# An attention and density kernel on one core: the values' offset written by ScalarE, later output stores, and a denser last stretch

## The chip, the core and the metric

The kernel runs on one core of a Trainium2 chip. TensorE (PE) multiplies matrices into PSUM; VectorE (DVE), ScalarE (ACT) and GpSimd (POOL) work element by element; SyncE (SP) issues nearly all DMAs here. Each engine works through its own instructions in order, and semaphores tie the engines together. The metric is the device time in microseconds (us) of one execution.

## What is computed

The input `x` has 8 images of 192 channels and 64 x 64 points. Layer 0 is attention over the 4096 points of an image, added to x; layer 1 is a per-channel density, added again:

```python
# layer 0, on g = group_norm(x)
q = prelu(conv1x1(g, w1, b1), a1)        # 24 channels
k = prelu(conv1x1(g, w2, b2), a2)        # 24 channels
v = prelu(conv1x1(g, wa, ba), aa)        # 192 channels: the "values"
score = softmax(q^T k, axis=2)           # 4096 x 4096
x = x + score @ v
# layer 1, on xr = group_norm(x), a small net per channel (1, 3, 3, 3, 1 units)
lower, upper = net(xr - 0.5), net(xr + 0.5)
sign = -sign(lower + upper)
x = x + maximum(abs(sigmoid(sign * upper) - sigmoid(sign * lower)), 1e-6)
```

All data is float32. A float32 matmul of the program shows as two records in the profile.

## The kernel before

**Steps.** An image's attention is 8 row blocks of 512 queries (n) by 16 steps; `t` counts the steps of all images, 1024 in all, `t % 16` is the step within a row block, and `b` is the image. In a step the loop at the end of the function calls `scores(t + 1)`: two matmuls (L802) into the one `sc` tile and, on ACT, the exponential (L806) into one of two `e` tiles. Then `max_step(t + 22)`: two matmuls (L729) and a maximum on DVE (L737) for a later row block. Then `attend(t)`: eight matmuls (L817, sixteen records) that add `e` times the values to the output of the row block. Then `work_off(t)` runs everything else. The last 22 steps have no `max_step` any more.

**Work written by hand into an order.** `at(t, fn, cost, act, pe)` puts a function into step t; `run_due` runs those that are due. What needs a PSUM bank is a `job`: `start_job` starts at most one a step when a bank of the tile in `homes` is free (the one of the two `turns` tiles b0 and b1, of two banks each, that `attend` is not adding into), from step 3 of a row block, and only when its hold fits before step 16. A job keeps its banks for `hold` further steps. Jobs are: `keys` (L641: queries and keys of 256 points), `values`, the output's transposes and residual (`finish`: L850, L859), the group norm (`norm_end`) and the folding of norm and weights (`weights`).

**Values.** A value job makes 256 points by 192 channels: two banks, three channel groups (L690, 64 rows each), and as a fourth product a row of ones times `ba`, the offset, which so reaches every point:

```python
for g in range(4):
    for s in range(2):
        ... lhsT=t[p, g, k * 128 : k * 128 + 128] if g < 3 else one_row[p],
            rhs=wf["v", b][p, g, :] if g < 3 else wf["ba", b][p],
```

One step later two activations on ACT (L617) and, after them, one DVE instruction (L620) make the prelu. An image has 16 value jobs; image 0's run in the head, before the steps, and those of image b + 1 mostly in the steps of image b. `wf["ba", b]` is made in `weights` from `ba_row`, which holds the offset in two of its 128 partitions (L200, L226, L587).

**SP's queue.** SP issues in order: loads of x for statistics, keys and values (`load`, L109, xi), of x for the residual (L109, xc, three tiles of 4 row blocks each), the keys' and queries' stores and reloads (L656, L657, L672), the row maxima (`max_end`: collected at step 9, `nd<-rn` L769 at step 11, `q<-nd` L774 at step 13, needed by the scores of the next row block) and the output (L1382). In `store` the DVE instruction that adds the density to xc (L1379) and the two output DMAs are in the same step; after an xc tile's last third its buffer is free, and a load that was held back for it follows in that step.

**Density.** 12 units an image (2 halves of the points x 3 channel groups x 2 bounds), each a list of instructions for DVE and ACT (L1102 `stt` on DVE; L1070, L1079, L1085, L1095 on ACT). `density_step` gives them out step by step against a credit on each engine; DVE's rate is what is left of the oldest image's units over the steps to its end plus 15, at most `MOST` = 3.3 us a step. `ending` joins two units and leads to `store`. After the last step image 6's rest is worked off, and image 7's units run with part of their sums on PE (L1041, the "tail"), some onto banks that ACT has filled (L1025).

**Head.** The x of image 0 is loaded, 14 matmuls of the identity (L146, tile `idle`) run meanwhile, then norm, keys and values of image 0.

Of the kernel before, what the change touches and what calls it, by code (L numbers as in the profile page):

```python
# [17 lines left out]
def kernel(  # L18
# [43 lines left out]
    nc = tc.nc  # L62
# [78 lines left out]
    make_identity(nc, ident)  # L141


    idle = ps_mx.tile([128, 2, F], F32, tag="mx", name="idle")
    for i in range(14):
        nc.tensor.matmul(  # L146
            idle[:, i % 2, 0:384], lhsT=ident, rhs=ident.unsqueeze(1).to_broadcast([128, 3, 128]),
            start=True, stop=True,
        )
# [27 lines left out]
    ba_row = const.tile([128, C], F32, name="ba_row")  # L177
# [3 lines left out]
    for t in (*wr, ba_row, one_row):  # L181
        nc.vector.memset(t, 0.0)
    nc.vector.memset(one_row[0:1], 1.0)
    nc.vector.memset(one_row[R : R + 1], 1.0)
# [10 lines left out]
    for s in range(2):  # L195
        p = slice(R * s, R * s + R)
        nc.scalar.dma_start(out=s1[p], in_=w1t.rearrange("(r g) o -> r g o", g=3))
        nc.scalar.dma_start(out=s2[p], in_=w2t.rearrange("(r g) o -> r g o", g=3))
        nc.scalar.dma_start(out=sa[p], in_=wat.rearrange("(r g) o -> r g o", g=3))
        nc.scalar.dma_start(out=sb[R * s : R * s + 1], in_=ba.unsqueeze(0))  # L200
    for i in range(2):
        for k in range(4):
            b_ = b2 if k // 2 == i else b1
# [8 lines left out]
    def spread():  # L212

        for i in range(2):
            for k in range(4):
                at = slice(32 * k, 32 * k + CR)
                p = slice(R * (k % 2), R * (k % 2) + R)
                nc.gpsimd.tensor_copy(wr[i][p, :, at], (s2 if k // 2 == i else s1)[p])
        for g in range(3):
            nc.gpsimd.tensor_copy(  # L220
                wa_sb[:, g, :].rearrange("p (h r) -> p h r", h=3),
                sa[:, g, :].rearrange("p (r h) -> p h r", h=3),
            )
        for s in range(2):
            p = slice(R * s, R * s + 1)
            nc.gpsimd.tensor_copy(  # L226
                ba_row[p].rearrange("p (h r) -> p h r", h=3),
                sb[p].rearrange("p (r h) -> p h r", h=3),
            )

    def negatives():
        for i, a in enumerate((*slope, vslope)):
# [101 lines left out]
    def at(t, fn, cost=0.0, act=0.0, pe=0.0):  # L334

        due.setdefault(max(t, now[0]), []).append((fn, cost, act, pe))
# [24 lines left out]
        ps_mx.tile([128, 2, F], F32, tag="mx", name="mx_head"),  # L361
    ]

    scratch = []
    for k in "ab":
        pair = []
# [5 lines left out]


    spot = [None]

    def spotted():

# [10 lines left out]
    def start_job(t):  # L388
        p = t % STEPS
        for n, (rank, make, hold, banks, cols) in enumerate(jobs):  # L390
            if stream[0] and (p < 3 or p + max(hold, 1) >= STEPS):
                continue
            rooms = [(pm, g) for pm, g in homes if sum(k <= t for k in g) >= banks]
            if not rooms:
                if rank < 2:
                    return
                continue
            k = [i for i in (1, 0) if ready[i] <= t and scratch[i][0].shape[1] >= cols]
            if cols and not k:
                continue  # L400
            del jobs[n]
            pm, guest = min(rooms, key=lambda r: max(r[1]))
            at_ = [i for i in range(2) if guest[i] <= t]
            for i in at_[:banks]:
                guest[i] = t + hold + 1
            if cols:
                ready[k[0]] = t + 2
            spot[0] = next(n for n, k in enumerate(turns + others) if k is pm), at_[0]
            parts = make(pm if banks == 2 else pm[:, at_[0], :], scratch[k[0]] if cols else None)
            for i, fn, cost, act, pe in parts:  # L410
                at(t + i, fn, cost, act, pe)
            return
# [50 lines left out]
    def norm_end(key, n, t, then=None):  # L463
# [68 lines left out]
                then()  # L532

        def make(pm, _):
            cell["pm"] = pm
# [12 lines left out]
    def weights(b, then):  # L548
# [41 lines left out]
        at(now[0] + 1, scale, 0.3, 2.0)  # L590

        def make(pf, _):
            cell["pf"] = pf
            cell["write"], cell["read"] = spotted()
            return [(0, products, 0.0, 0.0, 2.0), (1, offsets, 1.0, 0.0, 0.0)]
# [34 lines left out]
    def keys(b, d, what, done):  # L630
# [5 lines left out]
        def make(pk, u):  # L636
            if b not in kt:
                kt[b] = kpool.tile([128, N // 4], F32, tag="k", name=f"k_{b}")
            write, read = spotted()
            for g in range(3):  # L640
# [36 lines left out]

    def values(b, d, k, what, done):

        t = xi[what, b, d]  # L680
        c, h = divmod(d, 2)

        def make(pv, u):
            if (b, c) not in vt:
                vt[b, c] = vtiles.pop(0)
            v = vt[b, c][:, :, 2 * h + k, 0:C]
            for g in range(4):
                for s in range(2):
                    p = slice(R * s, R * s + R)
                    nc.tensor.matmul(  # L690
                        pv[:, s, 0:C],
                        lhsT=t[p, g, k * 128 : k * 128 + 128] if g < 3 else one_row[p],
                        rhs=wf["v", b][p, g, :] if g < 3 else wf["ba", b][p],
                        start=g == 0, stop=g == 3,
                    )
# [12 lines left out]

    rowmax = {}
# [118 lines left out]
    def finish(b, n, t):  # L828
# [17 lines left out]
        def turn():  # L846
            po = cell["po"]
            for k in range(2):
                for g in range(3):
                    nc.tensor.transpose(  # L850
                        po[:, g, k * 128 : k * 128 + 128],
                        o[k][:, g].rearrange("p s r -> p (s r)"), ident,
                    )

        u = slice((n % 4) * 256, (n % 4) * 256 + 256)
# [11 lines left out]
                norm_end((b, 1), 3 * NB, now[0] + 1, lambda: density(b))  # L867

        def make(po, _):
            cell["po"] = po.rearrange("p a (j c) -> p (a j) c", j=2)  # L870
            return [(0, turn, 0.0, 0.0, 1.3), (1, residual, 1.0, 0.0, 0.0)]

# [422 lines left out]
    def ending(b, c, g):  # L1295
# [80 lines left out]
        def store(parts=(slice(0, 2 * F),)):  # L1376
            for n in parts:
                x_ = xc[b, c][:, g, n]
                nc.vector.scalar_tensor_tensor(x_, z[0][:, n], 1e-6, x_, ALU.max, ALU.add)  # L1379
                for i in range(2):  # L1380
                    k = i * N // 2 + c * 2 * F
                    nc.sync.dma_start(  # L1382
                        out=ov[b, :, g, k + n.start : k + n.stop], in_=x_[R * i : R * i + R]
                    )
            bufs.append(z[0])
            if g == 2:
                xc.pop((b, c))
                free["xc"] += 1

# [134 lines left out]
    for t in range(last):  # L1524
# [9 lines left out]
                diagonals(2, last - 11)  # L1534
        now[0] = t
        if t % STEPS == 0:
            homes[:] = [(turns[(t // STEPS + 1) % 2], [0, 0])]
        if 3 < t < IMG:
            next(rest, None)
        assert t != IMG or next(rest, 0) == 0  # L1540
# [49 lines left out]
```

## Time and profile before

| what | value |
|---|---|
| median of 3 runs | 4759.76 us (4755.29 to 4764.86) |
| the profiled execution | 4759.02 us; its span 4757.2 us |
| mean granted TensorE clock | 0.985 |
| head: to the first L817 | 0 to 92.3 us |
| the 1024 steps | 92.3 to 4414 us |
| tail | 4414 to 4757 us |
| PE busy in 92 to 4414 us | 4301 of 4322 us |
| ACT and DVE busy in 92 to 4414 us | 2944 and 3775 us |
| SP's longest waits | L769 for DVE 1251.6 us in all, L1382 for DVE 894.8 us, L656 for DVE 671.3 us |

In the profile a group's line has the source line, engine, operation, what is written and read, the shape, the number of records, then busy time, the mean in ns of one, and the idle time just ahead with what ended it. A timeline line begins with the start and the duration in us. A window's line has the stretch, its length, then busy time and count for PE, PE's weight loads, DVE, ACT and POOL, the granted clock, the DMA share and GB/s. A wait of SP in its queue is often no more than SP being early.

### The profile page before, as it was taken

The page shows a single profiled execution, that of the slowest core. Times are in us where ns is not written, and L with a number is a line of the kernel's source. Part 1 is how long each engine was busy: PE and PEld are TensorE (multiplying, and loading weights), DVE is VectorE, ACT ScalarE, POOL GpSimd, SP SyncE. Part 2 cuts the span into 40 slices and gives each one's busy share as a digit, 9 for nine tenths or more (in the row PEclk, how much of TensorE's full clock was granted, in tenths as well). Part 3 has the DMA queues.
Part 4 walks back from the last instruction along what each step waited for, and adds up shares of the span by engine and source line. Part 5 has one row for each costly group of instructions (what it writes and reads, how often), then busy time and mean ns, then how long its engine had stood idle before and what let it go on. Part 6 is the DMA issues. An engine that isn't in the chain of part 4 may idle for free.

```text
span 4757.2 us, 68763 instructions
## 1 busy us (share of the span) xinstructions
PE 4609.7 (97%) x28116; PEld 3403.4 (72%) x28116; DVE 4125.5 (87%) x4161; ACT 3218.6 (68%) x3687; POOL 869.8 (18%) x841
## 2 busy tenths in 40 slices
PE   8999999999999999999999999999999999999685
PEld 5777777777777777777777777777777777777332
DVE  5433359999999999999999999999999998998898
ACT  2333247777677767877777767777777777778786
POOL 0000001222122212321212312222222222232100
PEclk9999999999999999999999999999999999999797
DMA  2101010111100111110111111111111101001000
GB/s 62 39 19 30 19 45 18 36 24 33 47 22 25 38 40 34 28 34 19 36 47 25 30 41 36 24 29 33 36 36 36 24 23 27 10 6 23 9 14 14
DMA packets 144145, 139.25 MB, mean 29 GB/s; under 512 B 51410, under 2 KB 116948, under 8 KB 143828
## 3 DMA queue, kind: packets, MB, share of 16 engines
q1 hardware_dynamic: 142592, 134.47, 12.1%
q8 instruction: 221, 3.62, 0.4%
q14 instruction: 96, 0.79, 0.1%
q10 hardware_dynamic: 1236, 0.37, 0.0%
HBM read 101.10 MB, written 29.49 MB: 27 GB/s over the span
## 4 chain that ended last, share of the span: by engine, by line
PE 89%; DVE 5%; ACT 3%; DMA 2%; issue 1%; SPq 0%; POOL 0%; ACTq 0%; POOLq 0%; DVEq 0%
PE b L817 57%; PE sc L802 21%; PE b L690 4%; DVE d L1102 3%; PE b L641 2%; PE b L1041 1%; PE mx L729 1%; DMA q<-nd 1%; PE mx_tail L1041 1%; PE b L850 1%; DVE rm L737 1%; DMA out_dram<-xc 0%; ACT d L1095 0%; PE sc_tail L1041 0%; SPq L109 0%
## 5 line engine op out<-in xcount | busy, mean ns | idle before, releaser
L817 PEld LDWEIGHTS b<-v,e 128*128 128x128 f32 x16384 | 2651.8, 190 | 777.8 <-issue 767.2
L817 PE MATMUL b<-v,e 128*128 128x193 f32 x16384 | 2955.6, 334 | 0.0
L806 ACT ACTIVATE e<-sc 128x1024 f32<-128x1024 f32 x1024 | 1044.7, 1020 | 1333.2 <-PE mx L729 1300.1
L737 DVE TENSOR_REDUCE rm<-mx 128x1 f32<-128x1024 f32 x1002 | 1224.1, 1222 | 511.6 <-PE mx L729 499.3
L802 PE MATMUL sc<-q,k 25*128 25x512 f32 x4096 | 1157.7, 641 | 23.6 <-DMA q<-nd 17.6
L729 PE MATMUL mx<-k,q 24*128 24x512 f32 x4008 | 1131.6, 641 | 0.0
L1102 DVE SCALAR_TENSOR_TENSOR d<-d,lc,d 128x1024 f32<-128x1024 f32 x756 | 977.3, 1301 | 17.2 <-ACT d L1079 4.8
L1102 DVE SCALAR_TENSOR_TENSOR d<-d,wsp,d 128x1024 f32<-128x1024 f32 x684 | 877.6, 1285 | 45.3 <-ACT d L1095 36.3
L1285 POOL MEMSET pause<- 128x1 f32 x408 | 40.0, 98 | 3560.9 <-DVE d L1102 3560.9
L1102 DVE SCALAR_TENSOR_TENSOR d<-d,tf,d 128x1024 f32<-128x1024 f32 x540 | 685.2, 1291 | 1.9 <-ACT d L1085 1.8
L1085 ACT ACTIVATE d<-d 128x1024 f32<-128x1024 f32 x540 | 567.2, 1052 | 38.0 <-DVE d L1102 37.7
L802 PEld LDWEIGHTS sc<-q,k 25*128 25x128 f32 x4096 | 308.1, 183 | 253.3 <-issue 205.8
L1095 ACT ACTIVATE d<-d,cb,wsp 128x1024 f32<-128x1024 f32 x348 | 429.9, 1235 | 1.5 <-DVE d L1102 0.6
L1070 ACT ACTIVATE d<-xc,bn,wn 128x1024 f32<-128x1024 f32 x288 | 354.2, 1234 | 0.8 <-issue 0.8
L1133 POOL TENSOR_TENSOR d<-d,d 128x512 f32<-128x512 f32 x168 | 340.9, 2029 | 45.9 <-ACT d L1127 44.8
L1079 ACT ACTIVATE d<-xc,bn,wn 128x1024 f32<-128x1024 f32 x252 | 311.1, 1234 | 0.0
L729 PEld LDWEIGHTS mx<-k,q 24*128 24x128 f32 x4008 | 300.0, 183 | 8.1 <-DVE rm L737 7.5
L1332 POOL TENSOR_TENSOR d<-d,d 128x512 f32<-128x512 f32 x80 | 172.5, 2156 | 0.0
L1320 POOL TENSOR_TENSOR d<-d,d 128x512 f32<-128x512 f32 x80 | 167.2, 2091 | 0.0
L1340 POOL TENSOR_TENSOR d<-d,d 128x512 f32<-128x512 f32 x80 | 159.5, 1994 | 2.0 <-POOL pause L1285 0.3
L690 PE MATMUL b<-wv,xi 64*128 64x192 f32 x1344 | 139.5, 340 | 0.0
L690 PEld LDWEIGHTS b<-wv,xi 64*128 64x128 f32 x1344 | 106.5, 186 | 25.4 <-issue 25.2
(156 smaller groups left out, 2176.9 us busy)
## 6 DMA issues: line engine op xcount, KB each, us to landing
xi<-in_x_dram SPq DMA_DIRECT2D x280, 192.0 KB
xc<-in_x_dram SPq DMA_DIRECT2D x64, 384.0 KB
out_dram<-xc SPq DMA_DIRECT2D x94, 256.0 KB
q<-qd SPq DMA_DIRECT2D x128, 128.0 KB
k<-kq SPq DMA_DIRECT2D x64, 64.0 KB
qd<-kq SPq DMA_DIRECT2D x64, 64.0 KB
q<-nd SPq DMA_DIRECT2D x256, 2.0 KB
d<-in_x_dram SPq DMA_DIRECT2D x16, 192.0 KB
```

The source lines that it names most:

```text
L690: nc.tensor.matmul(pv[:, s, 0:C], lhsT=t[p, g, k * 128 : k * 128 + 128] if g < 3 else one_row[p], rhs=wf["v", b][p, g, :] if g < 3 else wf ...
L729: nc.tensor.matmul(sc[:, s, :], lhsT=tile_of(qt[b, n // 2], n, j)[r], rhs=kt[b][r, u : u + F], start=True, stop=True,)
L737: nc.vector.tensor_reduce(out=rowmax[b, n][:, j, k : k + 1], in_=sc, axis=AX.XY, op=ALU.max)
L802: nc.tensor.matmul(sc[:, s, :], lhsT=kt[b][r, k : k + 128], rhs=qt[b, n // 2][r, :, u : u + 256], start=True, stop=True,)
L806: return lambda: nc.scalar.activation(e, sc, AF.Exp)
L817: nc.tensor.matmul(a[:, j, 0 : C + 1], lhsT=e[:, s, j * 128 : j * 128 + 128], rhs=v[:, s, p % 4, :], start=p == 0 and s == 0 and j % 2 == ...
L1070: nc.scalar.activation(self.buf[k], self.src(), AF.Tanh, bias=bn[:, s, g, 0, i : i + 1], scale=wn[:, g, 0, i : i + 1],)
L1079: nc.scalar.activation(self.buf[k], self.src(), AF.Identity, bias=bn[:, s, g, 1, i : i + 1], scale=wn[:, g, 1, i : i + 1],)
L1085: nc.scalar.activation(self.buf[k], self.buf["l", k[1], k[2]], AF.Tanh)
L1095: nc.scalar.activation(self.buf[k], self.buf["l", n - 1, 0], AF.Identity, bias=offset, scale=wsp[:, g, w : w + 1],)
L1102: nc.vector.scalar_tensor_tensor(dst, src, factor, dst, ALU.mult, ALU.add)
L1133: return nc.gpsimd.tensor_tensor(z[:, n], z[:, n], dst[:, n], ALU.add)
```

## The change

Value jobs that are neither image 0's nor of the last quarter of an image's values (`at_once`) let ACT write the offset into both banks in one step; the products run a step later, three groups instead of four, and add to what stands there. The job holds its banks and scratch tiles a step longer, so `start_job` asks for a step more. Whether a product adds or overwrites depends on what earlier matmuls of the bank left, so `part` notes banks where it may not, the warming matmuls now touch all eight banks (16 of 512 columns, for 14 of 384), and the output's transposes set the start flag only once a bank. For ACT's write the offset must stand in all partitions: `ba_all` is loaded by one broadcast DMA. The output's DMAs of a `store` are issued two steps after its DVE instruction, up to 12 steps before the last; the buffer comes free then. In the last 22 steps DVE's density rate aims at 8 steps after the last and may reach 4.3.

```diff
-    idle = ps_mx.tile([128, 2, F], F32, tag="mx", name="idle")
-    for i in range(14):
-        nc.tensor.matmul(
-            idle[:, i % 2, 0:384], lhsT=ident, rhs=ident.unsqueeze(1).to_broadcast([128, 3, 128]),
...
-        nc.scalar.dma_start(out=sb[R * s : R * s + 1], in_=ba.unsqueeze(0))
+    nc.scalar.dma_start(out=sb, in_=ba.partition_broadcast(128))
...
+    for i in range(16):
+        pm = (turns + others)[i // 2 % 4]
+        nc.tensor.matmul(
+            pm[:, i % 2, :], lhsT=ident, rhs=ident.unsqueeze(1).to_broadcast([128, 4, 128]),
+            start=True, stop=True,
+        )
...
-            if stream[0] and (p < 3 or p + max(hold, 1) >= STEPS):
+            if stream[0] and (p < 3 or p + max(hold, 1) + (cols > P and hold) >= STEPS):
...
-                ready[k[0]] = t + 2
+                ready[k[0]] = t + 2 + (banks == 2 and hold)
...
-            cell["read"](nc.vector.tensor_tensor(d, ba_row, pf[:, 4 : 4 + C], ALU.subtract))
+            cell["read"](nc.vector.tensor_tensor(d, ba_all, pf[:, 4 : 4 + C], ALU.subtract))
...
+        at_once = what == "first" or what == "v" and c == ORDER[3]
...
+            both = {(spot[0][0], i) for i in range(2)}
+            onto = not at_once and not part & both
+            part.difference_update(both)
+
+            def offset():
+                if onto:
+                    nc.scalar.activation(
+                        pv[:, :, 0:C], wf["ba", b].unsqueeze(1).to_broadcast([128, 2, C]), AF.Copy
                     )
-            done()
+
+            def products():
+                for g in range(4 - onto):
...
+                            start=not onto and g == 0, stop=g == 3 - onto,
+                            skip_group_check=onto,
+                        )
+                done()
...
+            if at_once:
+                products()
+                return [
+                    (0, lambda: None, 0.0, 0.0, 1.4), (1, first, 0.0, 1.1, 0.0),
+                    (2, last, 0.62, 0.0, 0.0),
+                ]
             return [
-                (0, lambda: None, 0.0, 0.0, 1.4), (1, first, 0.0, 1.1, 0.0),
-                (2, last, 0.62, 0.0, 0.0),
+                (0, offset, 0.0, 0.55, 0.0), (1, products, 0.0, 0.0, 1.1),
+                (2, first, 0.0, 1.1, 0.0), (3, last, 0.62, 0.0, 0.0),
             ]
 
-        job(make, *((0, 1) if what == "v" else (k, 3)), 2, 2 * C)
+        job(make, 0 if at_once else 1, 1 if what == "v" else 3, 2, 2 * C)
...
-                for g in range(3):
-                    nc.tensor.transpose(
+                for g in (1, 0, 2):
+                    nc.tensor.matmul(
                         po[:, g, k * 128 : k * 128 + 128],
-                        o[k][:, g].rearrange("p s r -> p (s r)"), ident,
+                        lhsT=o[k][:, g].rearrange("p s r -> p (s r)"), rhs=ident,
+                        is_transpose=True, start=k == 0 and g > 0, stop=True,
...
+            if t + LEAD >= last:
+
+                rate = min(left * COST["DVE"] / (last + 8 - t) + OTHER, MOST + 1.0)
...
                 nc.vector.scalar_tensor_tensor(x_, z[0][:, n], 1e-6, x_, ALU.max, ALU.add)
-                for i in range(2):
...
+                if now[0] >= last - 12:
+                    send(n)
             bufs.append(z[0])
-            if g == 2:
+            if now[0] < last - 12:
+
+                at(now[0] + 2, send)
...
+        def send(n=slice(0, 2 * F)):
+            x_ = xc[b, c][:, g, n]
+            for i in range(2):
+                k = i * N // 2 + c * 2 * F
+                nc.sync.dma_start(
+                    out=ov[b, :, g, k + n.start : k + n.stop], in_=x_[R * i : R * i + R]
+                )
+            if g == 2 and now[0] < last - 12:
+                xc.pop((b, c))
                 free["xc"] += 1
```

More of the change, by code (lines that the diff above doesn't have):

```diff
@@ L141 @@
     make_identity(nc, ident)
-    idle = ps_mx.tile([128, 2, F], F32, tag="mx", name="idle")
-    for i in range(14):
-        nc.tensor.matmul(
-            idle[:, i % 2, 0:384], lhsT=ident, rhs=ident.unsqueeze(1).to_broadcast([128, 3, 128]),
-            start=True, stop=True,
-        )
     gavg = const.tile([128, 128], F32, name="gavg")
@@ L176 @@
     wa_sb = const.tile([128, 3, C], F32, name="wa_sb")
-    ba_row = const.tile([128, C], F32, name="ba_row")
+    ba_all = const.tile([128, C], F32, name="ba_all")
     one_row = const.tile([128, 128], F32, name="one_row")
@@ L180 @@
     nslope = const.tile([128, 3], F32, name="nslope")
-    for t in (*wr, ba_row, one_row):
+    for t in (*wr, one_row):
         nc.vector.memset(t, 0.0)
@@ L223, in spread @@
             )
[L224 to L229, printed above, removed]
+        nc.gpsimd.tensor_copy(
+            ba_all.rearrange("p (h r) -> p h r", h=3), sb.rearrange("p (r h) -> p h r", h=3)
+        )
     def negatives():
@@ L374 @@
     spot = [None]
+    part = set()
     def spotted():
@@ L534, in make @@
         def make(pm, _):
+            part.add(spot[0])
             cell["pm"] = pm
@@ L592, in make @@
         def make(pf, _):
+            part.add(spot[0])
             cell["pf"] = pf
@@ L639, in make @@
             write, read = spotted()
+            part.discard(spot[0])
             for g in range(3):
@@ L686, in make @@
             v = vt[b, c][:, :, 2 * h + k, 0:C]
[L687 to L694, printed above, removed]
-                    )
-            done()
+            both = {(spot[0][0], i) for i in range(2)}
[5 more added lines that the diff above has]
+                        pv[:, :, 0:C], wf["ba", b].unsqueeze(1).to_broadcast([128, 2, C]), AF.Copy
+                    )
+            def products():
+                for g in range(4 - onto):
+                    for s in range(2):
+                        p = slice(R * s, R * s + R)
+                        nc.tensor.matmul(
+                            pv[:, s, 0:C],
+                            lhsT=t[p, g, k * 128 : k * 128 + 128] if g < 3 else one_row[p],
+                            rhs=wf["v", b][p, g, :] if g < 3 else wf["ba", b][p],
+                            start=not onto and g == 0, stop=g == 3 - onto,
+                            skip_group_check=onto,
+                        )
+                done()
             first, last = prelu(
@@ L848, in turn @@
             for k in range(2):
-                for g in range(3):
-                    nc.tensor.transpose(
+                for g in (1, 0, 2):
+                    nc.tensor.matmul(
                         po[:, g, k * 128 : k * 128 + 128],
-                        o[k][:, g].rearrange("p s r -> p (s r)"), ident,
+                        lhsT=o[k][:, g].rearrange("p s r -> p (s r)"), rhs=ident,
+                        is_transpose=True, start=k == 0 and g > 0, stop=True,
+                        skip_group_check=True,
                     )
@@ L869, in make @@
         def make(po, _):
+            part.difference_update((spot[0][0], i) for i in range(2))
             cell["po"] = po.rearrange("p a (j c) -> p (a j) c", j=2)
@@ L1379, in store @@
                 nc.vector.scalar_tensor_tensor(x_, z[0][:, n], 1e-6, x_, ALU.max, ALU.add)
-                for i in range(2):
[L1381 to L1384, printed above, removed]
-            bufs.append(z[0])
-            if g == 2:
+                if now[0] >= last - 12:
+                    send(n)
+            bufs.append(z[0])
+            if now[0] < last - 12:
+                at(now[0] + 2, send)
+            elif g == 2:
+                xc.pop((b, c))
[5 more added lines that the diff above has]
+                    out=ov[b, :, g, k + n.start : k + n.stop], in_=x_[R * i : R * i + R]
+                )
+            if g == 2 and now[0] < last - 12:
                 xc.pop((b, c))
@@ L1536 @@
         if t % STEPS == 0:
-            homes[:] = [(turns[(t // STEPS + 1) % 2], [0, 0])]
+            n = (t // STEPS + 1) % 2
+            homes[:] = [(turns[n], [0, 0])]
+            if t >= 2 * STEPS:
+                part.difference_update((n, i) for i in range(2))
         if 3 < t < IMG:
```

## The prediction

> **What bounds the kernel now.** I read the shares and slices of the page first, then its chain, then the groups, then the timeline of PE and of SP's queue around the longest waits.
>
> ```profile
> span 4757.2 us, 68763 instructions
> PE 4609.7 (97%) x28116; PEld 3403.4 (72%) x28116; DVE 4125.5 (87%) x4161; ACT 3218.6 (68%) x3687; POOL 869.8 (18%) x841
> PE   8999999999999999999999999999999999999685
> PE 89%; DVE 5%; ACT 3%; DMA 2%; issue 1%; SPq 0%; POOL 0%; ACTq 0%; POOLq 0%; DVEq 0%
> ```
>
> PE is busy from 92 us to 4414 us (the 1024 steps), and the chain agrees: 89% PE, DMA 2%. In the timeline the sixteen L817 matmuls of a plain step start every 3.88 us, and a step with more PE work is longer by just that work. So a matmul taken out of the steps is time saved, and ACT or DVE work there is free while it has room. After 4414 us that no longer holds.
>
> ```profile
> L690 PE MATMUL b<-wv,xi 64*128 64x192 f32 x1344 | 139.5, 340 | 0.0
> L690 PE MATMUL b<-ba,one_row 64*128 64x192 f32 x512 | 62.9, 322 | 0.0
> L806 ACT ACTIVATE e<-sc 128x1024 f32<-128x1024 f32 x1024 | 1044.7, 1020 | 1333.2 <-PE mx L729 1300.1 <-PE sc L802 30.0 <-ACT d L1095 0.2
> L617 ACT ACTIVATE pra<-b 128x384 f32<-128x384 f32 x128 | 55.7, 492 | 14.9 <-DVE v L620 12.5 <-DVE kq L620 2.4
> L802 PE MATMUL sc<-q,k 25*128 25x512 f32 x4096 | 1157.7, 641 | 23.6 <-DMA q<-nd 17.6 <-ACT e L806 5.7
> ```
>
> 512 records carry the offset row: 128 jobs, 4 records each (a written f32 matmul shows as two). PE's real waits in the steps are for q<-nd. SP's queue and PE at one of them:
>
> ```profile
> 4010.45 1.16 SPq L1382 DMA_DIRECT2D out_dram<-xc  x2
> 4014.68 2.56 SPq L109 DMA_DIRECT2D xc<-in_x_dram  x4
> 4017.27 0.60 SPq L769 DMA_DIRECT2D nd<-rn  x1
> 4029.37 2.39 SPq L774 DMA_DIRECT2D q<-nd  x4
> ```
>
> ```profile
> 4024.09 2.88 PE L817 MATMUL b<-v,e 128*128 128x193 f32 x16
> 4032.65 1.30 PE L802 MATMUL sc<-q,k 25*128 25x512 f32 x2 [5.68 <-DMA q<-nd]
> ...
> 4034.75 4.09 PE L817 MATMUL b<-v,e 128*128 128x193 f32 x16
> ```
>
> The load of a new xc tile must wait until the store that frees it has landed (4010.45 to 4014.68). Behind it in SP's queue stand nd<-rn, whose data was ready at 4005.6, and q<-nd, which PE needs at 4027.
>
> **Part 1: two matmuls less in 84 value jobs.** 7 images x 16 jobs less 4 that keep the old form: 84 jobs (the changed kernel's built order has 84 activations b<-ba). Each loses 4 records. Price: in the head two value jobs follow each other at 55.36 and 56.76, so 16 records take 1.40 us, 0.0875 each, 0.35 us for four. Ends: 0.32 (the offset's four at 56.44, next job at 56.76) and 0.42 (47.11 to 47.53, other work next). I take 0.35, the mean of a whole job: 84 x 0.35 = **-29.4 us** (-27 to -35).
>
> In exchange ACT writes 128x384 from SBUF to PSUM 84 times. No row has it; the nearest are 0.49 us (L617, PSUM to SBUF) and 0.61 us (L557, SBUF to SBUF, 128x384). At 1024 columns the write to PSUM of L1025 takes 1.10 against 1.23 to SBUF (L1070), so I take 0.49, 41 us of ACT. It is hidden by ACT's idle time ahead of the exponentials, 1333 / 1024 = 1.3 us a step. The new waits: PE's products, one step later, wait for that write, with the next step's scores queued behind them; the write is emitted a whole step ahead, so it is done. The write itself waits for the bank's last reader, with density work and a later exponential behind it on ACT. From the end of an exponential to the start of the scores that need its bank there are 1.62 us in the median; in images 1 to 7, 38 of 799 steps without a value job have under 0.5 us. So some 84 x 38/799 = 4 late exponentials, at up to 1.1 us (the step at 683.2 us is 1.03 long over the rule): **+2 us** (0 to +8).
>
> **Part 2: output stores two steps later.** Reading the L817 starts, I collect what the steps beside a late q<-nd are too long by: at 1296 and 1307 us 6.84 + 1.44; at 4024 and 4035 us 6.78 + 1.21; at 2123 and 2129 us 1.82 + 1.68; at 1578, 2669, 3213 and 3757 us 1.51, 1.40, 1.38, 1.46. Together 25.5 us, more than the 17.6 of the wait row, because matmuls after a long wait run slow: above, L802 1.30 for 0.70 and L817 4.09 for 2.88; the granted clock is 0.5 for 6.83 us from 4030.4. (The Trainium skill, "TensorE: Matmul & The Clock Gate", Part 1, says the clock halves after about 3.4 us idle and returns after as long a busy stretch; here a gap of 1.57 us at 2127.8 also brought 3.41 us at 0.5, so the trace is harsher. By that rule this pair would be worth 1.7 us less.)
>
> In the built order all seven have store and load ahead of q<-nd in the last steps before it is due: emitted at step 10, 11 or 12 of 16, q<-nd at 13. In the changed order six of the seven come at 14, after q<-nd. The seventh (image 7) moves from ahead of nd<-rn to behind it, with its DVE work two steps old, so SP need not wait. One new pair stands ahead of nd<-rn (image 1, sixth row block, step 10), two steps earlier relative to its data than the one shown above. I count 1 us for these (0 to 8): **-24.5 us** (-25.5 to -17). What else moves: xc comes free two steps later, so (image 3) its load is issued at step 414 instead of 411 and the first residual of the tile waits for the next turn of the banks (step 419 for 414). Its next user, the evacuation into the two o buffers, is at step 433; nothing on PE waits. Key jobs shift, and their stores now stand at steps 11 and 12 in five row blocks of images 2 to 6; one such pair before the change (step 318) cost nothing.
>
> **Part 3: more density in the last 22 steps.** In the built order 54 density and ending instructions of DVE fall there for 48, and 265 instead of 271 DVE instructions after the steps: six x 1.2 us (their spacing back to back) = 7.3 us moved. They fit: DVE is busy 71.4 of the 88 us from 4326, ACT 71.6 of 88 and gets five more. In the tail:
>
> ```profile
> 4414.00:4757.00 343.00, 234.68 (x503) 99.80 (x501) 297.91 (x274) 248.86 (x245) 11.02 (x10) 0.85 0.05 13
> ```
>
> DVE (third figure) is busy 298 of 343 us, but the tail's chain is DVE for only some 40%, PE 31% and ACT for much of the rest. 0.4 x 7.3 = **-3 us** (-7.3 to +5, if ACT comes late in those steps).
>
> **Part 4: the head.** Warming matmuls: 28 records of 384 columns from 1.36 us, 0.64 each until the clock rises at 6.1, then 0.32. 32 of 512 columns take 0.853 and 0.427: 4.74 us for 5.6 of them, 11.3 us for 26.4, end at 17.4. The first useful matmul waits for DVE's statistics until 23.07: **0**, hidden by them; without that cover up to 16 us. Between 27 and 34 us PE ran at clock 0.5; were the later end to keep it full, L568, L573 and the first L641 would win 1.3 + 1.05 + 0.66 = 3 us; the gap of 5.7 us argues against it. (The same section's 3.4 us window says cold as well.) The offset read into 128 partitions is 98 KB more, at the head's 76 GB/s 1.3 us, partly beside other work: **+0.5** (-3 to +1.3). Transposes are as many as before: 0.
>
> **Sum** against the profiled execution (4759.0 us: span 4757.2 and 1.8 around it): -29.4 + 2 - 24.5 - 3 + 0.5 = -54.4, 4704.6; the median of the runs is 0.7 higher, so 4705.
>
> **The rivals.**
> - *The late q<-nd stays*: another SP entry (a key job's store at step 12, the pair of image 1) takes the store's place. For: SP serves in order, and key jobs shifted. Against: the precedent at step 318. Part 2 falls away: 4705 + 24.5 = 4730. 13%.
> - *ACT comes late, slower*: the write and the two relus of two value jobs in neighbouring steps push the exponential past its 1.62 us, PE waits in each of the 84. At 1.1 us each +92: 4705 - 2 + 92 = 4795. It turns the sign from (54.4 + 2) / 84 = 0.67 us a job. For: ACT works 4.24 of the 5.38 us of a value step and 3.28 of 4.09 in the others, and the write goes into the latter. Against: density's credit on ACT is cut by the write's 0.55. 5%. (By the skill's rule gaps of 1.1 us would not cool the clock; one of five short waits here did.)
> - *The products save nothing*: accumulating on ACT's data runs slower, or PE hides the pair elsewhere. Against: in the tail L1041 onto banks that ACT filled runs at the same 0.43 us spacing. 4734. 5%.
> - *Better*: the head stays warm, the tail takes all 7.3 us, value at 0.42: 4705 - 3.5 - 4.3 - 5.9 = 4691. 7%.
>
> **How the numbers follow.** Forecast 67%, a mild form of the ACT rival (half a microsecond or so a job, near no change) 3%. Low: -35.3 - 25.5 - 7.3 - 3 = -71, 4688. High: the first rival with +5 from the tail, 4735. 0.2% (9.5 us) is about what a measurement of this kernel can tell from no change. Slower by more: the ACT rival, 5%; within: its mild form, 3%; faster: the rest, 92%.
>
> **What would show it.** After: L690 b<-ba at 176 records, 84 ACT writes near 0.49 us; plain steps still 3.88 us, value steps 5.38 - 0.35 = 5.03; L802 waiting for q<-nd under 3 us in all; steps from 92 us end near 4360; tail near 340 us. Wrong if L802 waits for L806 by tens of us, if q<-nd waits persist, or if value steps stay at 5.38.

## The result, and the profile after

The changed kernel takes 4706.68 us, the median of four runs (4706.02 to 4707.86), the kernel before 4762.31 us beside it (4755.29 to 4767.1): a ratio of 0.9885, 95% interval 0.9868 to 0.9902. Forecast were 4705 us in a range of 4688 to 4735. The total is right, in part by luck: of its terms one was seven microseconds too small, the others together were nearly nine too favourable, so the errors cancel, and a dependence between the parts was not seen. The page of the profile after, shares and chain:

```profile
span 4704.1 us, 68114 instructions
...
PE 4576.1 (97%) x27784; PEld 3371.2 (72%) x27784; DVE 4109.5 (87%) x4160; ACT 3260.4 (69%) x3771; POOL 869.5 (18%) x840
...
PE 89%; DVE 5%; ACT 4%; issue 1%; DMA 1%; POOL 0%; SPq 0%; POOLq 0%; ACTq 0%; DVEq 0%
```

PE has 33.6 us less work and the span is 53.1 us shorter: more than the removed products went. In the chain DMA is down from 2% to 1%. Groups that answer to those shown of before (L704 is the former L690, L828 the exponential L806, L824 the scores L802):

```profile
L824 PE MATMUL sc<-q,k 25*128 25x512 f32 x4096 | 1154.5, 640 | 13.3 <-ACT e L828 11.8 <-DMA q<-nd 1.2
L828 ACT ACTIVATE e<-sc 128x1024 f32<-128x1024 f32 x1024 | 1045.6, 1021 | 1227.0 <-PE mx L751 1202.3 <-PE sc L824 22.9
L704 PE MATMUL b<-wv,xi 64*128 64x192 f32 x1344 | 139.5, 340 | 0.0
L696 ACT ACTIVATE b<-ba 128x384 f32<-128x384 f32 x84 | 41.4, 493 | 1.8
L704 PE MATMUL b<-ba,one_row 64*128 64x192 f32 x176 | 21.6, 322 | 0.0
```

The offset's records are down from 512 to 176, and ACT writes 84 times at 0.493 us. The wait for q<-nd ahead of the scores fell from 17.6 to 1.2 us; the wait for the exponential rose from 5.7 to 11.8.

I divide each profiled span at the starts of the first and of the last L817 group (after: L839), and inside the steps I compare the distance between the starts of two steps with the median of the steps that have the same other PE work.

| stage | before | after | difference |
|---|---|---|---|
| head | 92.3 | 93.0 | +0.7 |
| steps, first to last L817 | 4319.7 | 4276.3 | -43.4 |
| tail | 345.2 | 334.9 | -10.3 |

A value step went from 5.382 to 5.057 us, so 84 of them are 27.3 us. The seven stretches around a late q<-nd were 25.5 us too long before; after, all are at their usual length but the one at step 926, which keeps 1.45. This is SP's queue and PE there, the place that the prediction showed at 4010 us of before:

```profile
3969.80 0.38 SPq L791 DMA_DIRECT2D nd<-rn  x1
3970.24 1.16 SPq L1422 DMA_DIRECT2D out_dram<-xc  x2
3981.38 2.86 SPq L109 DMA_DIRECT2D xc<-in_x_dram  x4
3984.34 2.38 SPq L796 DMA_DIRECT2D q<-nd  x4
```

```profile
3986.58 2.88 PE L839 MATMUL b<-v,e 128*128 128x193 f32 x16
...
3991.31 0.89 PE L824 MATMUL sc<-q,k 25*128 25x512 f32 x2 [1.19 <-DMA q<-nd]
```

nd<-rn now leaves ahead of the store, as soon as its data is there. But the store, issued right behind nd<-rn, takes 11 us to land and not 4 (3970.24 to 3981.38, against 4010.45 to 4014.68 before; the last section comes back to it), and the load waits for it 9.9 us with q<-nd behind. At the other six places the pair stands behind q<-nd and PE waits for nothing.

What the steps gave back: at steps 408, 536, 664 and 792 there are 1.2 us each that were not there before (step 280 had them already), 4.8 us in all. On ACT's timeline at step 408:

```profile
1803.11 1.00 ACT L828 ACTIVATE e<-sc 128x1024 f32<-128x1024 f32 x1
1804.13 1.28 ACT L501 ACT_TABLE_LOAD   x1
1805.42 0.20 ACT L501 ACTIVATE sq<-ve 128x1 f32<-128x1 f32 x1
1805.64 1.28 ACT L1353 ACT_TABLE_LOAD   x1
1806.94 1.15 ACT L1353 ACTIVATE d<-d 128x512 f32<-128x512 f32 x2
1808.00 0.61 ACT L1355 ACTIVATE d<-d 128x512 f32<-128x512 f32 x1
1808.52 1.00 ACT L828 ACTIVATE e<-sc 128x1024 f32<-128x1024 f32 x1
```

```profile
1805.56 2.88 PE L839 MATMUL b<-v,e 128*128 128x193 f32 x16
1809.57 0.70 PE L824 MATMUL sc<-q,k 25*128 25x512 f32 x2 [1.13 <-ACT e L828]
```

The group norm's square root needs another table of functions: 1.28 us to load it and 1.28 to load the old one back, and in the new order both fall into the same step as an ending's tanh (L1353, L1355). Before, the square roots stood in these same steps, but the exponential came right behind them: it is the tanh that moved there. The exponential comes late; no write of the offset is near.

The tail, in the windows' view (busy us and count of PE, PE's loads, DVE, ACT and POOL, then clock, DMA share, GB/s), and the 22 steps ahead of it:

```profile
4372.00:4704.00 332.00, 228.32 (x499) 97.61 (x498) 287.52 (x267) 241.78 (x240) 6.33 (x8) 0.87 0.05 13
4284.00:4372.00 88.00, 88.00 (x466) 66.44 (x458) 79.85 (x65) 77.98 (x93) 25.23 (x24) 1.00 0.03 7
```

DVE and ACT are busy 80 and 78 of the 88 us, where it was 71 and 72; PE has no idle time there, so the moved work costs the steps nothing.

### The profile page after: what moved, and what is told of

It reads as the page before. It is cut to its first block, busy times and chain, and to the rows that moved or that the text cites. A ratio compares the mean times of both kernels' runs of the same rounds, so it can differ in the third digit from the quotient of the medians.

```text
span 4704.1 us, 68114 instructions
## 1 busy us (share of the span) xinstructions
PE 4576.1 (97%) x27784; PEld 3371.2 (72%) x27784; DVE 4109.5 (87%) x4160; ACT 3260.4 (69%) x3771; POOL 869.5 (18%) x840
## 4 chain that ended last, share of the span: by engine, by line
PE 89%; DVE 5%; ACT 4%; issue 1%; DMA 1%; POOL 0%; SPq 0%; POOLq 0%; ACTq 0%; DVEq 0%
PE b L839 58%; PE sc L824 22%; DVE d L1128 3%; PE b L704 3%; PE b L642 2%; PE b L1067 1%; PE mx L751 1%; PE b L873 1%; ACT d L1121 1%; ACT d L1111 1%; ACT e L828 1%; PE mx_tail L1067 0%; DVE rm L759 0%; ACT d L1105 0%; ACT d L1096 0%
## 5 line engine op out<-in xcount | busy, mean ns | idle before, releaser
L839 PEld LDWEIGHTS b<-v,e 128*128 128x128 f32 x16384 | 2647.7, 190 | 776.1 <-issue 767.8
L839 PE MATMUL b<-v,e 128*128 128x193 f32 x16384 | 2951.5, 334 | 0.0
L828 ACT ACTIVATE e<-sc 128x1024 f32<-128x1024 f32 x1024 | 1045.6, 1021 | 1227.0 <-PE mx L751 1202.3
L824 PE MATMUL sc<-q,k 25*128 25x512 f32 x4096 | 1154.5, 640 | 13.3 <-ACT e L828 11.8
L824 PEld LDWEIGHTS sc<-q,k 25*128 25x128 f32 x4096 | 306.4, 183 | 243.2 <-issue 199.2
L1105 ACT ACTIVATE d<-xc,bn,wn 128x1024 f32<-128x1024 f32 x252 | 310.9, 1234 | 0.0
L704 PE MATMUL b<-wv,xi 64*128 64x192 f32 x1344 | 139.5, 340 | 0.0
L1067 PE MATMUL b<-d,v 128*128 128x512 f32 x216 | 104.1, 635 | 30.2 <-ACT b L1051 26.7
```

Source lines behind the costliest of these rows:

```text
L704: nc.tensor.matmul(pv[:, s, 0:C], lhsT=t[p, g, k * 128 : k * 128 + 128] if g < 3 else one_row[p], rhs=wf["v", b][p, g, :] if g < 3 else wf ...
L824: nc.tensor.matmul(sc[:, s, :], lhsT=kt[b][r, k : k + 128], rhs=qt[b, n // 2][r, :, u : u + 256], start=True, stop=True,)
L828: return lambda: nc.scalar.activation(e, sc, AF.Exp)
L839: nc.tensor.matmul(a[:, j, 0 : C + 1], lhsT=e[:, s, j * 128 : j * 128 + 128], rhs=v[:, s, p % 4, :], start=p == 0 and s == 0 and j % 2 == ...
L1105: nc.scalar.activation(self.buf[k], self.src(), AF.Identity, bias=bn[:, s, g, 1, i : i + 1], scale=wn[:, g, 1, i : i + 1],)
```

## Experiments

Theory: the three parts do what the prediction says and add up; the queue's order decides on the late q<-nd. Rivals: ACT's write is paid after all; it is the time, not the order, of the stores that counts; the tail hides or does not hide the moved work. Times are medians, and ratios are to the kernel before, timed again beside each set (4760.2 to 4764.7 us); spans and steps come from the profiled execution of each.

**The three parts one by one.** First, the kernel before with the new `store` and `send` alone:

```diff
-                    nc.sync.dma_start(out=ov[...], in_=x_[R * i : R * i + R])
...
+                if now[0] >= last - 12:
+                    send(n)
...
+            if now[0] < last - 12:
+                at(now[0] + 2, send)
```

> The kernel before with the later output stores alone. Theory (each late q<-nd came from a store and load ahead of it in SP's queue, and only that): the excess of the seven stretches, 25.5 us, goes but for about 1.5 us, the 1024 steps take 4296 instead of 4320 us, plain and value steps keep 3.88 and 5.38 us, the tail keeps about 345 us; 4762 - 24 = 4738. Rival (the gap closed because the value jobs, and with them keys and loads, stand elsewhere): several of the seven waits stay; 4750 to 4762.

4736.14 us, ratio 0.9946 (0.9931 to 0.9961), steps 4296.7: as the theory said.

```profile
L802 PE MATMUL sc<-q,k 25*128 25x512 f32 x4096 | 1154.3, 640 | 6.8 <-ACT e L806 5.1 <-DMA q<-nd 1.4
```

The wait for q<-nd is 1.4 us instead of 17.6. Stretches of 3.3 us remain at step 926. Second, the changed kernel with the old stores and the old rate, that is the values alone:

```diff
-            if now[0] < last - 12:
-                at(now[0] + 2, send)
...
-            if t + LEAD >= last:
-                rate = min(left * COST["DVE"] / (last + 8 - t) + OTHER, MOST + 1.0)
```

> ScalarE's write of the offset with all that belongs to it (bank notes, warming matmuls, transposes, offset in all partitions), without the later stores and without the denser last stretch. Theory: 84 value steps of 5.06 instead of 5.38 us, 27.3 us less; waits for q<-nd of 15 to 28 us stay; tail near 345; 4762 - 27 = 4735, 4725 to 4742. Rival (the order of the value jobs also cures the late q<-nd): 4710 to 4718.

4789.6 us, ratio 1.0059 (1.0042 to 1.0076): slower than before, which neither theory allowed. The value steps are at 5.06 us as expected, so the 27 us are there. But the scores now wait 50.7 us for q<-nd. SP and PE at step 478, where before had 3.5 us too much and this has 8.6:

```profile
2106.15 1.12 SPq L1408 DMA_DIRECT2D out_dram<-xc  x2
2109.91 2.56 SPq L109 DMA_DIRECT2D xc<-in_x_dram  x4
2112.57 2.40 SPq L796 DMA_DIRECT2D q<-nd  x4
```

```profile
2111.37 2.88 PE L839 MATMUL b<-v,e 128*128 128x193 f32 x16
2119.85 1.39 PE L824 MATMUL sc<-q,k 25*128 25x512 f32 x2 [5.60 <-DMA q<-nd]
...
2122.04 4.70 PE L839 MATMUL b<-v,e 128*128 128x193 f32 x16
```

In before the store of this place left 9.1 us ahead of the step's L817 (2113.63 against 2122.73), here 5.2 us. In the built order the density's last DVE instruction on xc (L1408) stands one step later in row blocks 26 to 54 (named, here and in the expectations, by the row block whose queries q<-nd brings; it is issued in the one ahead), since the changed value jobs shift the order of the density around them. Ten stretches are 75.3 us too long, for 25.5. The steps nearly add up: 4319.7 - 27.3 + (75.3 - 25.5) + 4.8 for the four late exponentials = 4347.0; measured 4346.2.

Third and fourth, the rate alone on the kernel before, and the changed kernel without it (the same two lines added, or taken out):

```diff
+            if t + LEAD >= last:
+                rate = min(left * COST["DVE"] / (last + 8 - t) + OTHER, MOST + 1.0)
```

> The kernel before with the higher density rate in the last 22 steps alone. Theory A (the six moved VectorE instructions and their consequences explain the shorter tail, 345.2 to 334.9 us): steps unchanged at 4320 us, tail 335; 4752. Theory B (the rate is worth the 3 us of the prediction, the rest comes from where the density stands when the steps end): tail 341 to 343; 4759.

4750.44 us, ratio 0.9978 (0.9968 to 0.9987); the tail alone moved, from 345.2 to 335.8.

> The changed kernel without the higher density rate. Theory A (the rate made the tail shorter): tail 345, 4717. Theory B (it is worth 3 us): tail 338, 4710. Steps at 4276 us by both.

4722.16 us (4718.07 to 4725.36), ratio 0.9916 (0.9901 to 0.993), tail 345.4. By the tails the rate is worth 9.4 us alone and 10.5 with the other parts; by the medians 11.5 and 15.5, but 3 us of the latter lie in the head (96.0 us here, 93.0 in the changed kernel). The stores are not independent: alone they bring 26 us, with the values 4789.6 - 4722.2 = 67 us.

**Why the values alone are slower.** Three kernels for that. The kernel before with only the DVE instruction on xc one step later, values untouched:

```diff
-                later(2, store, 1.3)
+                later(3, store, 1.3)
```

> The kernel before, with the density's last DVE instruction on xc one step later and the store and the load with it; the values are as before (four products, no write by ACT). In the built order the pair then stands ahead of q<-nd at the same step as in the values-only kernel in row blocks 22 to 54. Theory A (it was this one step that cost the values-only kernel its gain, not the write by ACT): nine stretches of some 8 us each and the one at 926 remains: excess 75 to 86 us for 25.5, so 4810 to 4823. Rival B (the write by ACT or the changed order of the jobs makes q<-nd late): within 10 us of the kernel before, 4752 to 4772.

4822.89 us, ratio 1.0128 (1.0113 to 1.0143). One number, which changes no amount of work, costs 61 us:

```profile
L802 PE MATMUL sc<-q,k 25*128 25x512 f32 x4096 | 1165.7, 644 | 67.2 <-DMA q<-nd 60.7 <-ACT e L806 5.9
```

The wait for q<-nd is 60.7 us instead of 17.6, with no write by ACT in the kernel; the ten long stretches sum to 88 us. So that one step is what the values-only kernel lost by.

Next, values alone, stores at the old place, and only the freed xc tile announced two steps later, so that the load that waits for the store moves behind q<-nd:

```diff
-            if g == 2:
-                xc.pop((b, c))
-                free["xc"] += 1
+            if g == 2 and now[0] < last - 12:
+                at(now[0] + 2, leave)   # leave: the two lines above
```

> Only the value change of the kernel before, with the output stores in the step of their DVE instruction as before, but the xc tile counted as free two steps later, so that only the load that reuses it moves behind q<-nd. Theory A (q<-nd was held back by the load that waits in SP's queue for the store to land): the long stretches of the values-only kernel (78 us) go, 4789.6 - 70 = 4720, and L802 waits for q<-nd under 5 us in all. Rival B (the stores themselves, or their traffic, hold q<-nd back): 4760 to 4790, with q<-nd waits of 20 to 50 us.

4716.63 us, ratio 0.9903 (0.9889 to 0.9918):

```profile
L824 PE MATMUL sc<-q,k 25*128 25x512 f32 x4096 | 1154.5, 640 | 12.0 <-ACT e L828 11.8
```

No wait for q<-nd is left at all, at step 926 neither. It was the load, waiting at the head of SP's queue; the stores, still in the step of their DVE instruction, did no harm at these places.

Last, the stores alone on the kernel before, but one step later instead of two:

```diff
-                at(now[0] + 2, send)
+                at(now[0] + 1, send)
```

> The kernel before, with the output stores of the steps issued one step after their DVE instruction (not two). In the built order the store and the load that waits for it then still stand between nd<-rn and q<-nd in row blocks 22 to 54 of the steps, exactly as before; only at rows 18 and 50 (counted from 0) do they move behind q<-nd. Theory A (only the place in SP's queue counts, not the step in which the entry is written): the seven long stretches stay but the one at step 286 (8.3 us): 4762 - 8 = 4754, steps near 4311. Rival B (what counts is that the store comes later in time): most of the stretches shrink as with two steps, 4736 to 4742.

4753.26 us, ratio 0.9981 (0.9972 to 0.9991), steps 4311.2: the times that theory A gave, but by luck, since two things that it did not have cancel. Where the order of the queue is unchanged, SP does the same at the same time: in the last steps of row blocks 21 and 37 (L817 of steps 350 and 606) the starts of store, load and q<-nd, counted from that L817, agree with the kernel before within 0.03 us. Writing an entry a step later does nothing by itself; it has to pass another entry. The stretches at 286 and at 926, where the pair did pass an entry, went but for 0.7 us (15.6 us less; theory A had the first alone), and the five others grew by 7.5 in all. PE waits 0.2 to 0.9 us longer there: before, six transposes (L850, 0.65 us) stood ahead of the scores in each of these five steps, and in the new order they stand elsewhere, so PE comes sooner to a q<-nd that lands at about the same time (the scores start 4.4 to 4.9 us after the step's L817, before 4.7 to 5.1). After four of these waits, now 1.5 to 2.0 us and three of them under 1.3 before, L817 took 4.4 to 4.6 us instead of 2.88. The end on the clock below comes back to that.

**Is ACT's write hidden?** The changed kernel with each write made twice:

```diff
                     nc.scalar.activation(
                         pv[:, :, 0:C], wf["ba", b].unsqueeze(1).to_broadcast([128, 2, C]), AF.Copy
                     )
+                    # the same three lines again
```

> The changed kernel, with each of the 84 writes of the offset by ACT made twice (the second overwrites the first with the same numbers): 41 us more work on ACT in the steps, which no plan of the kernel counts. Theory A (ACT has room ahead of its exponentials, the writes are hidden): 4707 to 4714. Rival B (ACT is near its limit in these steps, every further half microsecond is paid): up to 84 x 0.49 = 41 us, 4735 to 4748.

4712.33 us (4709.62 to 4713.34), ratio 0.9892 (0.9875 to 0.9908):

```profile
L827 PE MATMUL sc<-q,k 25*128 25x512 f32 x4096 | 1155.3, 640 | 14.2 <-ACT e L831 11.8 <-DMA q<-nd 2.2
L699 ACT ACTIVATE b<-ba 128x384 f32<-128x384 f32 x84 | 41.5, 495 | 2.7
```

With the second write (L699) ACT works 41.5 us more, and the scores wait for the exponential 11.8 us as before. The steps are 3.4 us longer, 2.7 of them at step 926 for q<-nd; at most 0.8 us can be the writes'. The head of this execution was 3.1 us longer.

**More jobs in the new form.** The write also in the head:

```diff
-        at_once = what == "first" or what == "v" and c == ORDER[3]
+        at_once = what == "v" and c == ORDER[3]
```

> The changed kernel, with ACT writing the offset in the head's value jobs of image 0 too (16 more jobs, 100 writes in all). In the built order SP's queue in the steps is as in the changed kernel. Theory A (the head's value jobs are bound by PE's products there, as in the steps): 16 x 0.325 = 5.2 us off, 4701.5. Rival B (the head's end is set by other work, by DMAs or by ACT, which in the head has no idle exponentials to hide the write): 4706 to 4712.

4722.72 us, ratio 0.9914 (0.9901 to 0.9928): 16 us worse than the changed kernel, more than either theory had, and all of it in the head (109.2 us; steps 4275.4). The windows from 47 to 57 us, this kernel and then the changed one:

```profile
47.00:57.00 10.00, 9.40 (x42) 4.68 (x40) 6.94 (x8) 2.39 (x6) 0.00 (x0) 0.62 0.16 41
```

```profile
47.00:57.00 10.00, 9.75 (x82) 6.18 (x82) 8.78 (x10) 2.99 (x8) 0.00 (x0) 1.00 0.16 39
```

PE is busy in both, but at a granted clock of 0.62 it does half as many matmuls. From 45 us to the end of the head this kernel takes 64.2 us at a mean granted clock of 0.75, which is 48 us at full clock; the changed kernel takes 48.0 us at 1.00. So nearly all of the 16 us is the clock. In the head the write has no cover: near its end PE waits for it twice, 1.41 us each (98.0 and 101.7 us). Why the clock fell already at 49 us, after two waits of 0.5 and 0.6 us, stays open (the changed kernel has one of 0.7 there and keeps its clock).

The write in half of the last quarter's jobs as well (14 more), with the head's and then without:

```diff
-        at_once = what == "first" or what == "v" and c == ORDER[3]
+        at_once = what == "v" and c == ORDER[3] and h
```

> As the run with the head's jobs, and with the write also in half of the value jobs of the last quarter of each image: 14 more of them in the steps. The added step moves the density endings: in five row blocks (18, 26, 34, 42, 50) the store and its load stand ahead of q<-nd again, but their DVE instruction comes one step earlier than in the kernel before, where these rows cost nothing. Theory A (it is the time of that DVE instruction and the place in the queue that decide): no new wait, 14 x 0.325 = 4.6 us less than the run with the head alone. Rival B (any pair ahead of q<-nd costs 7 us or so): 30 to 40 us slower than that.

4701.62 us, ratio 0.9872 (0.9858 to 0.9885). The head is as bad as in the run before it (106.0 us), and the steps are 18.8 us shorter than there, not 4.6: the square roots no longer meet an ending's tanh, so the 1.2 us stretches are gone, and many small ones with them. The pairs ahead of q<-nd cost nothing in the five row blocks named, where their DVE instruction is early: theory A, and not every pair there is harmful. Two corrections: row block 18 did cost something in the kernel before (8.3 us at step 286), and one new wait, of 0.96 us, came at step 222.

The same with the release two steps later instead of the stores (the edit of the values-only kernel above):

```diff
-                at(now[0] + 2, send)
+                at(now[0] + 2, leave)
```

> As the run before it in this list, but stores in the step of their DVE instruction and only the xc tile's release two steps later, as in the run of the values alone with a later release. Theory A: the last stretch that is too long (step 926, 1.4 to 6 us in the runs with later stores) goes as well, 2 us less than with later stores, about 4694 if the head pays and 4699 if it does not. Rival B (the store ahead of nd<-rn delays the maxima): a wait for q<-nd at the five row blocks, 10 us or more slower.

4713.81 us, ratio 0.9894 (0.9881 to 0.9908): 12 us slower than with later stores, theory A's guess wrong and rival B's about right. In these row blocks, and at step 222 (row block 14), the store now stands ahead of nd<-rn and so delays the maxima themselves; at step 222 q<-nd is issued 1.8 us later than with later stores, and that stretch and the one at 542 are 6.9 and 5.7 us too long. Which of the two forms is better depends on the row block.

```diff
-        at_once = what == "first" or what == "v" and c == ORDER[3]
+        at_once = what == "first" or what == "v" and c == ORDER[3] and h
```

> The changed kernel, with the write by ACT also in half of the value jobs of the last quarter of each image (14 jobs more), and the head as in the changed kernel. By stages: head 93 to 96 as there, steps 4256.6 and tail 334.9 as in the run that had this and the head's jobs: span 4684.5 to 4687.5, median 4687 to 4690. Rival (the 20 us that the steps of that run were shorter came from its later start, not from the 14 jobs): 4702, the changed kernel less 14 x 0.325 = 4.6.

4692.37 us (4691.88 to 4693.13), ratio 0.9855 (0.9839 to 0.9872): the fastest of all, 14 us below the changed kernel. Head 93.5, steps 4263.1, tail 334.7. It lies between what the expectation (4687 to 4690) and its rival (4702) gave, nearer the first. The steps are 6.5 us longer than in the run with the head's jobs:

```profile
L824 PE MATMUL sc<-q,k 25*128 25x512 f32 x4096 | 1155.7, 640 | 8.1 <-DMA q<-nd 3.5 <-ACT e L828 2.8 <-ACT d L1105 1.7
```

Now q<-nd comes late at steps 222 and 926 (3.7 and 4.7 us too much with the slow matmuls behind). The profile puts the wait at 222 down to ACT (L1105), but the scores start there 7.1 us after q<-nd began to be issued, as in the run with the head's jobs (7.2), where it names q<-nd. Of the 13.2 us that the steps gain on the changed kernel 4.6 are the products' and the rest are stretches that vanished.

## Why the prediction was right, by its steps

| term | predicted | measured |
|---|---|---|
| products, 84 jobs | -29.4 | -27.3 |
| late exponentials | +2 | +4.8 |
| late q<-nd | -24.5 | -24.1 |
| other steps | 0 | +3.2 |
| head | +0.5 | +0.7 |
| tail | -3 | -10.3 |
| sum | -54.4 | -53.0 |

- **Products.** The records are 176 as foreseen, and four are worth 0.325 us, not 0.35. The step that failed is the price from a whole job of the head: its 16 records hold 12 of the three groups, and the offset's own four were the 0.32 that stood there as an end.
- **ACT's write.** 0.493 us, as estimated from the neighbouring rows, and hidden; the doubled write shows that it would be hidden twice over. The late exponentials exist, but the writes do not make them: the endings' tanh do, which moved into the steps of four square roots.
- **Late q<-nd.** The mechanism and its size are right: the stores alone brought 25.8 us, and removing only the load's wait cleared everything. Two steps of it failed. At step 926 SP need not wait, said the prediction; it waited 9.9 us, for a store that landed slowly behind nd<-rn, and 1.45 us were left where 1 us was allowed. And the prediction took the parts as separate: it compared the stretches of before with the changed order, and never asked what the value jobs alone do to the time of the endings. Without the later stores the change would have been slower than the kernel before (4789.6 us; with the 10 of the rate about 4780, an estimate that no run tried).
- **Tail.** The mis-sized term. Six DVE and five ACT instructions moved, as read from the order. But 0.4 is DVE's share of the chain over the whole tail, and the work was taken from its beginning, image 6's rest. From the last step's L817 to the first group of products (L1041) in the chain there were 77.9 us before (4412.00 to 4489.87): 50.3 DVE, 12.9 ACT, 7.5 issue, 6.5 POOL; some of it:

```profile
4439.72 1.23 ACT d L1095
4440.95 0.03 issue
4440.98 1.30 DVE d L1102
4442.30 3.73 DVE d L1102 x4
```

  DVE is two thirds of this stretch. The instructions that left had 8.5 us on DVE and 6.1 on ACT. After, the stretch is 68.6 us (4369.25 to 4437.82): 44.6 DVE, 14.0 ACT, 6.8 issue, 2.6 POOL. So of the 9.3 us that it gained 5.7 are DVE's, two thirds of what left, and 3.9 are POOL's, which the prediction had at nothing; why POOL's part shrank stays open. The tail keeps this lead to its end. The predicted end of -7.3 did not reach it either, since it counted DVE's work alone, at 1.2 us each.
- **Head.** The warming matmuls end at 18.3 us (17.4 foreseen), the first useful one starts at 23.65: hidden. The broadcast's price cannot be told: five executions with the old head took 92.3 to 95.5 us, six with the new one 93.0 to 96.1.
- **The rest of the signs.** Plain steps stayed at 3.88 us, value steps came to 5.06 (5.03 foreseen), the tail to 332 us in the prediction's stretch (340). The steps end at 4372 and not near 4360: the steps gave 8.5 us less than forecast, the tail 7.3 more. The +3.2 of other steps is the sum of many excesses of under 1 us each; its cause stays open.
- **Rivals.** None took place. "ACT comes late" is refuted by the doubled write, "the products save nothing" by the step times. "The late q<-nd stays" was the nearest: in the values-only kernel it happened threefold, by the very queue that it named.

## What to carry to other kernels

A small transfer that gates the critical engine should not stand in an in-order queue behind a load that waits for a store to land, unless that store leaves early enough; look at where in the queue it stands, since writing an entry later helped here only where it passed another. An edit that shifts a software schedule by one step can turn a gain of 27 us into a loss of 28: price each part with and without the others. Take a chain's share from the stretch that the work leaves, not from the whole stage.

## What was not expected of the hardware

The clock of PE. The fourteen profiles here hold, in the steps, 60 waits of PE of 0.5 to 1.25 us, and after none of them did the next L817 group take more than 2.88 us. Of 15 waits from 1.41 to 2.18 us eleven were followed by a slow group (3.8 to 5.3 us), and all of 24 waits from 2.78 us up. The Trainium skill, "TensorE: Matmul & The Clock Gate", Part 1, lets the clock fall after a window of about 3.4 us idle. In the steps here 1.41 us were enough once and 2.11 not always. A wait of PE under 1.3 us cost its length and at most 0.3 us more; one of 1.41 to 2.18 us mostly cost 1.8 to 1.9 us more than its length, and the longer ones 1.9 to 3.5 us more.

An output store (two DMAs of 256 KB) that left 8.3 us or more behind nd<-rn, 512 numbers of 4 bytes, let the load behind it go after 3.8 to 5.5 us. In the fourteen profiles fourteen such stores left 4.1 to 4.8 us behind nd<-rn and took 6.8 to 8.4 us, and six left 0.4 us behind it and took 11.1 to 12.0: none of these twenty landed sooner than 11.0 us after nd<-rn had left. That nd<-rn is what slows them was not tried by itself. And the same head differed by 3 us from one profiled execution to another.
